# First layer of a two-layer graph attention kernel: half of a chunk's second contexts is issued ahead of the sums of the next chunk

## The chip, the cores and the metric

The kernel runs on one core of one Trainium2 chip. The time is the device time of one execution in microseconds (us). Three runs of the kernel before took 4297.36, 4297.43 and 4297.71 us; the median is 4297.43 us.

The core has five engines with a queue each: TensorE (PE in the profile), VectorE (DVE), ScalarE (ACT), GpSimd (POOL) and SyncE (SP, which here only issues transfers). An instruction waits for others by semaphores; the instructions behind it in the same queue wait with it.

## The reference

There are 8 batches of 2048 rows with 256 features, and one adjacency matrix of 2048 by 2048. Each of two layers normalises the rows, applies a ReLU, runs an attention layer over the graph and adds the result to its input. The change is in the first layer, whose attention normalises each chunk of 256 keys on its own:

```python
q = (x @ Wq.T + bq).reshape(B, N, H, Dh).transpose(0, 2, 1, 3)   # H = 4 heads, Dh = 64
...
scores = jnp.einsum('bhnd,bhjcd->bhnjc', q, kc) / jnp.sqrt(jnp.asarray(Dh, dtype=q.dtype))
scores = jnp.clip(scores, -10.0, 10.0)
scores = jnp.where(mask == 0, jnp.asarray(-10.0, scores.dtype), scores)
attn = jax.nn.softmax(scores, axis=-1)            # over the 256 keys of chunk j
ctx = jnp.einsum('bhnjc,bhjcd->bhnd', attn, vc)   # summed over the 8 chunks
out = ctx @ Wo.T + bo
```

After that come a residual and a layer norm. The second layer is an attention with additive scores, a leaky ReLU and one softmax over all keys. The change doesn't touch it.

## The kernel before, in words

**Tiling.** The first layer runs over steps (b, qb, c): batch, block of 512 queries (`QB`), chunk of 256 keys. That is 8 x 4 x 8 = 256 steps, named n. The scores are kept transposed, with keys on the partitions, so a chunk is two tiles of 128 keys (k = 0 and 1), and for each tile there are two pairs of heads (hp): four tiles E of 128 x 1024 a step.

**One step.** The loop that starts near L732 works on three chunks at once. In the order in which a step issues them:

1. `contexts(0)` (L749) multiplies the weights of key tile 0 of chunk n by the values. It calls `weigh` (L456, its matmuls are L460) for part 0 and part 1 (the two halves of each head's 64 values); each part has four heads, and so four matmuls of 32 columns that run beside each other. Part p goes into the PSUM bank `both[p]`.
2. `advance()` may put in a piece of other work: projections to q, k, v and the output projection (L153), transposes of normalised rows (L156), the adjacency masks (L272).
3. `prepared(steps[n + 2])` issues the scores of chunk n + 2: four times `scores` (L435), each two matmuls of 64 rows (L440) into a PSUM pair, and on DVE one clamp with the mask (L448), which writes E and leaves the pair free. ACT then takes the exponentials of the first two E (L454).
4. The sums of chunk n + 1: `add_up` (L468) multiplies the added exponentials by ones, four matmuls of 32 columns (L471), into half of a PSUM pair. `divide` (L475) has ACT copy them to `s` (L478), and SP moves them to a small tile `sum` (L480).
5. The second half of `prepared`: the exponentials of the other two E on ACT, and on POOL two adds (L725) of the first tile's and the second tile's exponentials, for the next step's sums.
6. `contexts(1)` (L762) adds key tile 1 of chunk n into `both`, part 0 and then part 1.
7. `accumulate` (L493): DVE multiplies `both[0]` and `both[1]` by r, the reciprocals of chunk n (L498), and POOL adds the products to the accumulator of the block (L500).
8. `spread` (L483): DVE takes the reciprocals of `sum` (L485), SP writes them to HBM (`inv`, L487) and reads them back, four transfers, spread over the partitions as r (L490). They are used in step n + 1.
9. `advance()` or `tick()` again puts in other work. Rows' statistics on DVE (`row_stats`, L47 and L48) and normalised rows on ACT (L144) come from there too.

**What sets the order.** The order is written out by hand: each engine's queue has its instructions in the order in which the program issues them. `advance` and `tick` step through generators (`aside`, `quiet`) with due times in steps.

**Buffers that matter here.** There are three PSUM pairs (`pair()`), handed out in turn to the scores, the sums and the other work (`aux`); two banks `both`, one buffer each; ten tiles E; two tiles `add`; one tile s and one tile r. A step's four scores and its sums take five pairs in a row, so the fourth scores take the pair of the first, and the sums that of the second.

Of the kernel before, what the change touches and what calls it, by code (L numbers as in the profile page):

```python
# [51 lines left out]
def layers(  # L52
# [40 lines left out]
    def pair(dtype=F32):  # L93
        n = QB if dtype == F32 else 2 * QB
        return psum.tile([P, 2, n], dtype, tag="big", name="big", bufs=3)

    def banks(name):
        return [psum.tile([P, QB], F32, tag=f"both{k}", name=name) for k in range(2)]
# [6 lines left out]
    def heads_tile(name, tag, bufs=2):  # L105
        return big.tile([P, 2, QB], F32, tag=tag, name=name, bufs=bufs)
# [96 lines left out]
    def tick():  # L203
        moved = False
        for steps_of in list(quiet):
            got = next(steps_of, quiet)
            if got is quiet:
                quiet.remove(steps_of)
            moved = moved or got is not False
        return moved  # L210

    def advance(all_of=True):

        moved = all_of and tick()
        for steps_of in list(aside):
            got = next(steps_of, aside)
            if got is aside:
                aside.remove(steps_of)
            moved = moved or got is not False
            if got is None:  # L220
                if here[0] < 0:
                    aside.append(aside.pop(aside.index(steps_of)))
                break
        return moved

    def drain(until=lambda: False):
        while not until() and advance():
            pass
# [54 lines left out]
    def other_limits():  # L283
        for qb in range(1, NQB):
            yield from make_limit(qb)
# [58 lines left out]
    def batch(b):  # L344
        qkv[b] = ([], [], [])
        rstd, off = norm_of[b] = norms()
        mv = small.tile([P, NKT, 2], F32, tag="mv", name="mv", bufs=1)
        ready, turned = [], []

        def slot():  # L350

            n = here[0]
            while b and here[0] < n + 1:
                yield False

        def statistics():

            for blk in range(NQB):
                while (
                    here[0] < first_of(b) + TURN[blk] - 2 or len(turned) < blk  # L360
                    if b
                    else blk > len(turned) + 1
                ):
                    yield False
                xb = load(x[b], blk)
                yield True
                yield from slot()
                for t in range(NT):
                    row_stats(nc, small, mv[:, blk * NT + t, :], xb[:, t, :])
                roots(mv, rstd, off, slice(blk * NT, (blk + 1) * NT))  # L370
                yield from slot()
                ready.append(xb)

        quiet.append(statistics())
        for blk in range(NQB):
            while len(ready) <= blk:
                yield False
            yield from block(b, blk, ready[blk], turned, *qkv[b])
# [77 lines left out]
    def weigh(kt, part, es, vs, both, first):  # L456

        for h in range(H):
            mine = slice(h * DH + 32 * part, h * DH + 32 * part + 32)
            nc.tensor.matmul(  # L460
                both[part][32 * h : 32 * h + 32, :],
                vs[kt // NT][:, kt % NT, mine],
                es[h // 2][:, h % 2, :],
                start=first,
                stop=not first,
            )

    def add_up(es, sums):  # L468

        for h in range(H):  # L470
            nc.tensor.matmul(  # L471
                sums[32 * h : 32 * h + 32, :], ones, es[h // 2][:, h % 2, :], start=True, stop=True
            )

    def divide(sums):  # L475

        s = big.tile([P, QB], F32, tag="s", name="s", bufs=1)
        nc.scalar.copy(s, sums)  # L478
        got = small.tile([P, 16], F32, tag="sum", name="sum")
        nc.sync.dma_start(got, s[0:P:32, :].rearrange("h (j i) -> h j i", i=16))  # L480
        return got

    def spread(got):  # L483

        nc.vector.reciprocal(got, got)  # L485
        held = dram.tile([H, QB], F32, tag="inv", name="inv", bufs=3)
        nc.sync.dma_start(held.rearrange("h (j i) -> (h j) i", i=16), got)  # L487
        r = big.tile([P, QB], F32, tag="r", name="r", bufs=1)
        for h in range(H):
            nc.sync.dma_start(r[32 * h : 32 * h + 32, :], held[h, :].partition_broadcast(32))  # L490
        return r

    def accumulate(acc, both, r, first):  # L493

        to = acc if first else heads_tile("c", "c")

        for part in range(2):
            nc.vector.tensor_tensor(to[:, part, :], both[part], r, ALU.mult)  # L498
        if not first:
            nc.gpsimd.tensor_tensor(acc, acc, to, ALU.add)  # L500
# [187 lines left out]
    def fill(qb):  # L688

        while here[0] < (B - 1) * NQB * NCH + qb * NCH + NCH - 1:  # L690
            yield False
        for two in range(NKT // 2):
            mine = limit[:, qb, 2 * two : 2 * two + 2, :]
            nc.scalar.activation(mine, mine, AF.Relu, scale=2.0 * FULL, saturate=False)
            yield True

    def last_batch():
        yield from batch(B - 1)
        yield from sources_of(W, a)
        yield from preparation(0)  # L700
# [9 lines left out]
    def prepared(step):  # L710


        b, qb, c = step
        drain(lambda: qb in made and b in qkv and len(qkv[b][1]) > c // 2 and len(qkv[b][0]) > qb)
        qs, ks, _ = qkv[b]
        tiles = [[scores(qb, 2 * c + k, hp, qs, ks) for hp in range(2)] for k in range(2)]
        for e in tiles[0]:
            exponential(e)
        yield tiles
        for e in tiles[1]:  # L720
            exponential(e)
        added = []
        for hp in range(2):
            both = heads_tile("add", "add")
            nc.gpsimd.tensor_tensor(both, tiles[0][hp], tiles[1][hp], ALU.add)  # L725
            added.append(both)
        yield added
# [3 lines left out]
    for n in range(-2, len(steps)):  # L731
        here[0] = n  # L732
        if n >= 0:
            b, qb, c = steps[n]
            if n == 0:
                aside.append(other_limits())
            b1 = 1 if n == 1 else b + 2 if (qb, c) == (NQB - 1, NCH - 2) else B
            if b1 < B:
                aside.append(batch(b1) if b1 + 1 < B else last_batch())
            if b == B - 1 and c == NCH - 2:  # L740
                aside.append(fill(qb))
            drain(lambda: len(qkv[b][2]) > c // 2)
            both = banks("both")

            def contexts(k):
                for part in range(2):
                    weigh(2 * c + k, part, weights[n][0][k], qkv[b][2], both, k == 0)

            contexts(0)  # L749

        used[0] = 0
        advance(n < 0)
        coming = prepared(steps[n + 2]) if n + 2 < len(steps) else iter(())
        weights[n + 2] = [next(coming, None)]
        inside = -1 <= n < len(steps) - 1
        if inside:
            sums = pair()[:, 0, :]
            add_up(weights[n + 1][1], sums)
            got = divide(sums)
        weights[n + 2].append(next(coming, None))  # L760
        if n >= 0:
            contexts(1)  # L762
            if c == 0:
                accs[qb] = heads_tile("acc", "acc")
            accumulate(accs[qb], both, r, c == 0)
            weights.pop(n)
            if c == NCH - 1:
                quiet.append(finish(b, qb, accs[qb]))
        if inside:
            r = spread(got)  # L770
        if n < NQB * NCH or used[0] == 0 or qb == NQB - 1 or qb == 0 and c < NCH // 2:
            advance()
        else:
            tick()
# [128 lines left out]
    for s, (k, jt) in enumerate(rounds):  # L903
# [31 lines left out]
        while due and due[0][0] <= s:  # L935
            _, m, parts = due.pop(0)
# [316 lines left out]
```

## Time and profile before

| | |
|---|---|
| median of three runs | 4297.43 us |
| the profiled execution | 4298.93 us, its span 4297.1 us |
| granted TensorE clock | 0.99 of full speed over the span |
| first layer's loop | from about 45 to 2780 us |
| PE / DVE / ACT / POOL busy from 60 to 2780 us | 2639 / 1849 / 1566 / 2138 us of 2720 |
| PE / DVE / ACT / POOL busy from 2780 to 4297 us | 1427 / 1337 / 934 / 1260 us of 1517 |

In a group's line the engine comes after the source line, then the operation with out<-in by the program's names, shapes, how many, busy time, mean duration in ns, and the idle time just ahead of them with what ended it. In a timeline a row has its start, its duration, engine, line, operation and how many records it merges. An fp32 matmul shows as two records, called passes here; the records of matmuls that run side by side start within some ns of each other. A matmul's record of about 0.59 us runs past the start of the next, so gaps on PE are read between starts. PEld is PE's weight load, SPq an issue of a transfer by SP; data land later than the issue ends.

### The profile page before, as it was taken

What the parts mean: (1) busy time and instruction counts of PE and PEld (TensorE: products, weight loads), DVE (VectorE), ACT (ScalarE), POOL (GpSimd) and SP (SyncE); (2) the same over time, 40 slices, a digit from 0 to 9 for tenths busy, and PEclk for the clock granted to TensorE, in tenths of its full rate; (3) what the DMA queues carried; (4) which work ended last, traced back from release to release, by engine and by line L of the source; (5) the groups of instructions that cost most, each with busy time, mean ns of one, the idle gap of its engine ahead of it and who ended that gap; (6) DMA issues with size and microseconds to landing.
All of it is one profiled execution on the core that took longest, in us unless ns stands there. A gap on an engine that the chain in (4) does not pass through costs nothing. (4 is left out here: it accounts for less than half of the span.)

```text
span 4297.1 us, 86491 instructions
## 1 busy us (share of the span) xinstructions
PE 4103.1 (95%) x34742; PEld 1452.8 (34%) x34742; DVE 3221.3 (75%) x3974; ACT 2527.1 (59%) x3194; POOL 3409.1 (79%) x1795
## 2 busy tenths in 40 slices
PE   7889999999999999999999999989999999999998
PEld 3333333333333333333333333323333233333322
DVE  4676766666667666666666567689898898988997
ACT  4555555555655565555555567565666656566665
POOL 2467787887788788788788778878887888887897
PEclk9999999999999999999999999999999999999999
DMA  3221121122112111112211121211221212122121
GB/s 100 81 90 49 47 59 57 47 55 60 47 54 62 49 52 54 57 47 54 61 49 52 59 61 46 86 57 52 60 70 33 75 52 67 53 59 70 33 62 34
DMA packets 280267, 248.16 MB, mean 58 GB/s; under 512 B 95792, under 2 KB 230704, under 8 KB 279856
## 3 DMA queue, kind: packets, MB, share of 16 engines
q1 hardware_dynamic: 275248, 225.76, 18.7%
q0 software_dynamic: 4608, 16.78, 1.0%
q8 instruction: 275, 4.51, 0.5%
q14 instruction: 136, 1.11, 0.1%
HBM read 204.15 MB, written 36.18 MB: 56 GB/s over the span
## 5 line engine op out<-in xcount | busy, mean ns | idle before, releaser
L448 DVE SCALAR_TENSOR_TENSOR E<-big,limit 128x1024 f32<-128x1024 f32 x1024 | 1182.7, 1217 | 653.3 <-PE big L440 647.1
L725 POOL TENSOR_TENSOR add<-E 128x1024 f32<-128x1024 f32 x512 | 1203.5, 2372 | 569.8 <-PE both L460 474.2
L454 ACT ACTIVATE E<-E 128x1024 f32<-128x1024 f32 x1024 | 1055.0, 1057 | 540.3 <-DVE E L448 521.9
L809 DVE SCALAR_TENSOR_TENSOR e<-big,far,limit 128x1024 f32<-128x1024 f32 x1024 | 1239.6, 1275 | 39.5 <-POOL t L928 18.3
L928 POOL TENSOR_TENSOR t<-t,e 128x1024 f32<-128x1024 f32 x448 | 1055.2, 2388 | 226.7 <-ACT t L924 225.6
L820 PE MATMUL acc<-e,qn 128*32 128x512 f32 x8192 | 1035.6, 596 | 5.6 <-DVE e L809 5.5
L440 PE MATMUL big<-qT,kT 64*128 64x512 f32 x4096 | 966.8, 609 | 43.0 <-DVE E L448 35.6
L460 PE MATMUL both<-E,v 128*32 128x512 f32 x8192 | 991.9, 596 | 0.5 <-DVE c L498 0.2
L924 ACT ACTIVATE t<-e,quot 128x1024 f32<-128x1024 f32 x512 | 561.4, 1142 | 267.9 <-PE big L832 165.0
L440 PEld LDWEIGHTS big<-qT,kT 64*128 64x128 f32 x4096 | 366.3, 187 | 589.9 <-issue 384.1
L500 POOL TENSOR_TENSOR acc<-acc,c 128x1024 f32<-128x1024 f32 x224 | 530.3, 2368 | 1.4 <-DVE c L498 1.4
L460 PEld LDWEIGHTS both<-E,v 128*32 128x32 f32 x8192 | 274.9, 110 | 601.8 <-issue 345.7
L820 PEld LDWEIGHTS acc<-e,qn 128*32 128x32 f32 x8192 | 274.5, 110 | 504.8 <-issue 462.0
L832 PE MATMUL big<-t,for_sums 128*32 128x512 f32 x2048 | 359.3, 596 | 62.3 <-POOL t L928 51.1
L498 DVE TENSOR_TENSOR c<-both,r 128x512 f32<-128x512 f32 x448 | 308.8, 690 | 44.3 <-PE both L460 17.3
L471 PE MATMUL big<-add,ones 128*32 128x512 f32 x2048 | 282.7, 610 | 12.2 <-DVE E L448 1.8
L478 ACT COPY s<-big 128x512 f32<-128x512 f32 x256 | 150.1, 586 | 81.2 <-PE big L471 81.1
L832 PEld LDWEIGHTS big<-t,for_sums 128*32 128x32 f32 x2048 | 76.2, 109 | 282.2 <-POOL t L928 172.2
L164 ACT COPY hT<-big 128x512 f32<-128x512 f32 x128 | 74.2, 580 | 135.2 <-PE big L156 135.2
L144 ACT ACTIVATE h<-x,off,rstd 128x256 f32<-128x256 f32 x256 | 139.1, 592 | 4.7 <-POOL off L135 4.7
L337 ACT ACTIVATE qT<-big,bq 128x512 f32<-128x512 f32 x64 | 44.0, 687 | 153.9 <-PE big L153 153.9
L318 ACT COPY v<-big 128x512 f32<-128x512 f32 x64 | 37.4, 584 | 157.4 <-PE big L153 120.1
(116 smaller groups left out, 3122.3 us busy)
## 6 DMA issues: line engine op xcount, KB each, us to landing
r<-inv SPq DMA_DIRECT2D x1024, 64.0 KB
x<-in_x_dram SPq DMA_DIRECT2D x96, 512.0 KB
es<-er SPq DMA_DIRECT2D x64, 512.0 KB
adj_in<-in_adj_dram SPq DMA_DIRECT2D x32, 512.0 KB
x<-o POOLq DMA_DIRECT2D x32, 512.0 KB, 3.3
x<-x SPq DMA_DIRECT2D x32, 512.0 KB
xh<-x SPq DMA_DIRECT2D x64, 256.0 KB
out_dram<-xh SPq DMA_DIRECT2D x64, 256.0 KB
```

The lines of the kernel that those rows point to most:

```text
L440: nc.tensor.matmul(ps[:, hh, :], ks[kt // NT][own, hp, (kt % NT) * P : (kt % NT + 1) * P], qs[qb][own, hp, :], start=True, stop=True,)
L448: nc.vector.scalar_tensor_tensor(e, ps, -0.5, bcast(limit[:, qb, kt, :], 1, 2), ALU.max, ALU.min)
L454: nc.scalar.activation(e, e, AF.Exp, scale=0.25 * EDGE)
L460: nc.tensor.matmul(both[part][32 * h : 32 * h + 32, :], vs[kt // NT][:, kt % NT, mine], es[h // 2][:, h % 2, :], start=first, stop=not first,)
L498: nc.vector.tensor_tensor(to[:, part, :], both[part], r, ALU.mult)
L500: nc.gpsimd.tensor_tensor(acc, acc, to, ALU.add)
L725: nc.gpsimd.tensor_tensor(both, tiles[0][hp], tiles[1][hp], ALU.add)
L809: nc.vector.scalar_tensor_tensor(e, near[hh], far[:, jt, h : h + 1], limit[:, 2 * half : 2 * half + 2, jt, :], ALU.max, ALU.min,)
L820: nc.tensor.matmul(acc[blk][32 * q : 32 * q + 32, :], qn[jt // NT][:, jt % NT, hp * P + 32 * q : hp * P + 32 * q + 32], es[q // 2][:, blk, :],
L832: nc.tensor.matmul(den[32 * q : 32 * q + 32, :], for_sums[:, m, 2 * hp + q // 2, :], ts[q // 2][:, q % 2, :], start=(m == 0 and k == 0), s ...
L924: nc.scalar.activation(t, now[hh], AF.Copy, scale=quot[:, jt // 2, h : h + 1])
L928: nc.gpsimd.tensor_tensor(ts[hh], ts[hh], now[hh], ALU.add)
```

## The change

`contexts` takes the parts that it is to do. Part 0 of the second key tile is issued ahead of the sums of chunk n + 1 (behind the scores of chunk n + 2), and part 1 stays where it was, behind the second half of `prepared`. On PE a step's order goes from scores, sums, part 0, part 1 to scores, part 0, sums, part 1. No matmul is added or taken out, and no other engine's instructions change places.

```diff
             both = banks("both")
 
-            def contexts(k):
-                for part in range(2):
+            def contexts(k, parts=range(2)):
+                for part in parts:
                     weigh(2 * c + k, part, weights[n][0][k], qkv[b][2], both, k == 0)
 
             contexts(0)
...
         inside = -1 <= n < len(steps) - 1
+        if n >= 0:
+            contexts(1, (0,))
         if inside:
             sums = pair()[:, 0, :]
             add_up(weights[n + 1][1], sums)
             got = divide(sums)
         weights[n + 2].append(next(coming, None))
         if n >= 0:
-            contexts(1)
+            contexts(1, (1,))
             if c == 0:
                 accs[qb] = heads_tile("acc", "acc")
             accumulate(accs[qb], both, r, c == 0)
```

## The prediction

> **What bounds the kernel now.** I read the page first, then the timeline of all engines over two steps of the first layer, then the whole first layer step by step. The page (its engine summary and its table of groups) says where time is spent:
>
> ```profile
> PE 4103.1 (95%) x34742; PEld 1452.8 (34%) x34742; DVE 3221.3 (75%) x3974; ACT 2527.1 (59%) x3194; POOL 3409.1 (79%) x1795
> ...
> L460 PE MATMUL both<-E,v 128*32 128x512 f32 x8192 | 991.9, 596 | 0.5 <-DVE c L498 0.2
> ...
> L471 PE MATMUL big<-add,ones 128*32 128x512 f32 x2048 | 282.7, 610 | 12.2 <-DVE E L448 1.8
> L478 ACT COPY s<-big 128x512 f32<-128x512 f32 x256 | 150.1, 586 | 81.2 <-PE big L471 81.1
> ```
>
> TensorE looks full, but its row hides short waits, because a matmul's record runs past the start of the next. So I read starts, in the timeline of the changed loop (start, duration, engine, line):
>
> ```profile
> 1317.74 3.70 PE L440 MATMUL big<-qT,kT 64*128 64x512 f32 x16
> 1318.99 4.62 DVE L448 SCALAR_TENSOR_TENSOR E<-big,limit 128x1024 f32<-128x1024 f32 x4 [1.57 <-PE big L440]
> ...
> 1321.49 1.06 PE L471 MATMUL big<-add,ones 128*32 128x512 f32 x8
> ...
> 1322.35 3.84 PE L460 MATMUL both<-E,v 128*32 128x512 f32 x32
> ...
> 1322.68 0.59 ACT L478 COPY s<-big 128x512 f32<-128x512 f32 x1 [0.25 <-PE big L471]
> ...
> 1323.17 2.01 ACT L454 ACTIVATE E<-E 128x1024 f32<-128x1024 f32 x2
> ...
> 1323.30 0.55 SPq L480 DMA_DIRECT2D sum<-s  x1
> ...
> 1323.52 1.50 DVE L498 TENSOR_TENSOR c<-both,r 128x512 f32<-128x512 f32 x2
> ...
> 1324.26 0.16 PEld L460 LDWEIGHTS both<-E,v 128*32 128x32 f32 x8 [0.89 <-DVE c L498]
> ...
> 1325.13 0.25 DVE L485 RECIPROCAL sum<-sum 128x16 f32<-128x16 f32 x1
> ```
>
> One step of 8.37 us (1317.74 to 1326.11) is a loop over two engines: scores on PE, four E on DVE, two c behind them, and the next contexts(0), which need `both` back from c, then the next scores. PE waits twice. (1) The last scores pass begins at 1317.74 + 3.70 - 0.59 = 1320.85 and the sums at 1321.49: 0.64 later, where passes otherwise follow at 0.43. (2) contexts(0) begins at 1324.26, right after the first c ends (1323.52 + 0.69 = 1324.21), 0.2 us after PE could have.
>
> **What the change moves.** Nothing is added or removed: per step the same four score pairs, four sums and eight contexts matmuls. Four contexts matmuls (one part, 1.72/2 = 0.86 us) go ahead of the four sums. Only PE's order changes; DVE, ACT, POOL and SP issue the same instructions in the same order. What changes for them is when the sums end.
>
> **Gain: the wait ahead of the sums.** The sums take a PSUM pair that the second E of this chunk must leave. E two ends at 1318.99 + 1.13 + 1.22 = 1321.34, and the sums begin 0.147 us later; in nearly all steps it is the same 0.147, so E is what ends this wait. Contexts part 0 needs no such tile: it can start as soon as the scores are out. How soon? The Trainium skill (TensorEngine Tiling (Array Packing), Key Properties) says that a change of tiling mode drains TensorE, and scores (64 rows) to sums or contexts (128 rows by 32 columns) is such a change. Taken as the whole of 0.64, the rule makes the gain zero, as the contexts meet it instead. A step where E two was early shows how much is drain:
>
> ```profile
> 53.91 5.09 PE L440 MATMUL big<-qT,kT 64*128 64x512 f32 x16
> 58.93 1.06 PE L471 MATMUL big<-add,ones 128*32 128x512 f32 x8
> ```
>
> There the last pass starts at 53.91 + 5.09 - 0.59 = 58.41 and the sums 0.52 later (0.52 also in the step at 170.29). So 0.09 is drain and 0.12 the wait for E. I take the row: 0.115 us a step where the gap is 0.635, 0.045 where it is 0.565.
>
> It counts only where nothing later catches it. In 147 of 253 steps contexts(0) follows contexts(1) at once and waits for c (wait 2, 0.2 us), whose time follows from the scores, not from the sums: gain 0. In 106 steps projection, transpose or output work lies between, and PE runs on. Summed over these, the gap above 0.52 is 13.4 us (53 steps at 0.63, 22 at 0.56 to 0.57, 12 at 0.68, five at 0.95); 1 us of that ends in the waits below. Gain: **12.4 us**.
>
> **Loss: everything behind the sums is later by 0.86 - 0.115 = 0.74 us** (0.81 where the gap is 0.565). The chain is: copy of s (ACT, idle and waiting for the sums in 249 of 256 steps), transfer to `sum`, reciprocal, transfer to `inv`, four transfers to r. Two queues stand behind it.
>
> *ACT*: exponentials three and four are behind the copy, so they, and what ACT does after them, move by 0.74. Usually PE doesn't care. It does where the rows of h for a transpose come right behind them:
>
> ```profile
> 2525.87 2.01 ACT L454 ACTIVATE E<-E 128x1024 f32<-128x1024 f32 x2
> ...
> 2527.77 0.58 ACT L164 COPY hT<-big 128x512 f32<-128x512 f32 x1
> 2528.24 1.09 ACT L144 ACTIVATE h<-x,off,rstd 128x256 f32<-128x256 f32 x2
> 2529.34 0.66 PE L156 MATMUL big<-ident,h 128*128 128x128 f32 x4
> ```
>
> ACT runs without a gap from exponential three to the second h (2528.24 + 1.09 = 2529.33), and the transposes begin at 2529.34. I find 14 transposes and 4 projections (waiting for hT) that end such an unbroken ACT run with a margin under 0.1 us: 18 x 0.77 = **13.8 us**. Ten further projections have 0.93 us: free.
>
> *DVE*: the reciprocal is bound by its transfer. In nearly every step it starts 1.84 to 1.93 us after that issue, with DVE idle 0.1 to 0.2 us before it, so it moves by the full 0.74. Normally 2 us of DVE idle follow. But where the statistics of rows (eight instructions, 2.1 us) stand behind it, the next chunk's first E waits:
>
> ```profile
> 1344.54 0.54 SPq L480 DMA_DIRECT2D sum<-s  x1
> ...
> 1346.44 0.25 DVE L485 RECIPROCAL sum<-sum 128x16 f32<-128x16 f32 x1 [0.17 <-DMA sum<-s]
> ...
> 1348.60 0.18 DVE L48 BATCH_NORM_AGGREGATE mv<-st 128x2 f32<-128x6 f32 x1
> 1348.70 2.32 DVE L448 SCALAR_TENSOR_TENSOR E<-big,limit 128x1024 f32<-128x1024 f32 x2
> ```
>
> The scores of that step began at 1347.36, so E could have started at 1347.36 + 1.25 = 1348.61; it starts at 1348.70, straight behind the statistics. Every delay of the reciprocal lands on E, c and the next contexts(0). There are 21 such steps with no slack: 9 x 0.81 + 7 x 0.74 + 5 x 0.70 = 16.0; in six, work between the contexts gives 0.13 back, and in four the transfer is already late (2.2 to 3.3 us) for another reason and may not move: 16.0 - 0.8 - 1.5 = **13.7 us**.
>
> *The rest.* Nine early steps (180 to 300 us) cast the adjacency masks on ACT behind the exponentials; between 0 and 9 x 0.74 = 6.7, taken as 3, as some wait for input. r lands some 2 us after its last issue (estimate from the one step at 1328.29 where the wait on DVE's queue is seen to end at 1330.31); c comes 3.6 us after that issue in a bare step, so 1.6 - 0.74 still covers it. Only four steps with SP held up have less: **1.6 us**. POOL's adds follow exponentials three and four and move by at most 0.74, and so do the sums that take them: the 0.8 us between stays. The accumulator's add (L500) and the output work stand behind POOL's adds, and SP's block loads behind its transfers; PE needs either a step or more later. Without this cover each bare step would pay up to 0.74.
>
> Sum: 13.8 + 13.7 + 3 + 1.6 - 12.4 = **+19.7 us**, all in the first layer; the second only shifts. The profiled execution took 4298.93 us (span 4297.1, 1.8 around it), the runs' median is 4297.43, 0.03% lower; I set the difference onto the median: **4317 us**.
>
> **Rivals.**
> - *Faster.* The 12.4 us come, and the delays don't bite, since ACT and DVE absorb them: 4285. For it: most DVE idle behind the reciprocal is 2 to 5 us. Against it: the 39 sites (18 + 21) with no margin. It decides once under 12.4/0.75 = 16 of the 39 really pay. 0.09.
> - *No change.* About half the sites pay, or part of each: 39 x 0.35 = 14 against 12.4: 4297 to 4302. 0.11.
> - *Drain takes all.* The skill's rule holds in full, gain zero: 4297.4 + 32.1 = 4330. The two steps at 0.52 speak against it. Within the slower side, 0.12.
> - *r becomes the bound* in bare steps (SP's queue delays it past c): with 0.3 us in each of 147 steps on top, 4317 + 44 = 4361. Against it: only two waits of c on r in the trace, 2.0 us in all. 0.04.
>
> **How the numbers follow.** My sum holds 0.64, drain 0.12, r 0.04: slower 0.80. Same (within 0.2% = 8.6 us, about what a measurement of this kernel can tell from no change) 0.11; faster 0.09. Ends: with half of the losses, 16 - 12.4 = +4 (4301); with the masks in full and four contended transfers moved too, +25; with drain, +33. A little past both: 4298 to 4332. Given slower, its own range is 4306 to 4332.
>
> **What would show it.** Right: in the timeline after, contexts (L460 x16) begins 0.52 after the last scores pass, sums follow 0.86 later, and the bare step stays at 8.37 with contexts(0) still released by c; the copy of s, reciprocal and exponentials three and four sit 0.74 later relative to the scores; the 8.30 us step with statistics behind it (1339.06) is followed by one of about 9.2 rather than 8.45; transposes like 2529.34 wait 0.74 for h; steps with work between contexts shorten by 0.1. The second layer's length stays. Wrong: bare steps change in length (then c isn't bound as I say), contexts starts 0.64 after the scores (drain), or the sites without margin keep their times.

## The result and the profile after

The changed kernel takes 4328.72 us (4324.22 to 4329.2, 4 runs) beside 4297.4 for the kernel before on the same chip: ratio 1.007, interval 1.0058 to 1.0083, slower by 31 us where 20 was forecast. Its profiled execution took 4328.3 us with a span of 4326.5, against 4298.93 and 4297.1. The lines of its page (engine summary and table of groups) that answer to those of before:

```profile
PE 4104.7 (95%) x34742; PEld 1391.9 (32%) x34742; DVE 3214.8 (74%) x3974; ACT 2526.0 (58%) x3194; POOL 3409.8 (79%) x1795
...
L460 PE MATMUL both<-E,v 128*32 128x512 f32 x8192 | 1037.9, 600 | 13.2 <-DVE c L498 2.2
...
L478 ACT COPY s<-big 128x512 f32<-128x512 f32 x256 | 150.0, 586 | 273.5 <-PE big L471 273.4
```

The counts are the same and PE, DVE, ACT and POOL are busy within 7 us of before, so nothing was added: the 31 us are waits. (The 46 us more in L460's row are the tail of one more group of records in each step, which overlaps the sums by 0.18 us.) One number stands out. ScalarE stands idle 273 us in front of the copy of `s`, where it stood 81 us before: 192 us more over 256 steps, 0.75 a step. That is the delay of the sums seen from ScalarE. In the timeline, the same step as the one shown before (its scores began at 1317.74 then):

```profile
1333.72 3.70 PE L440 MATMUL big<-qT,kT 64*128 64x512 f32 x16
...
1337.35 1.06 PE L460 MATMUL both<-E,v 128*32 128x512 f32 x8
1338.23 1.04 PE L471 MATMUL big<-add,ones 128*32 128x512 f32 x8
1339.09 3.06 PE L460 MATMUL both<-E,v 128*32 128x512 f32 x24
1339.41 0.59 ACT L478 COPY s<-big 128x512 f32<-128x512 f32 x1 [1.00 <-PE big L471]
...
1341.86 0.25 DVE L485 RECIPROCAL sum<-sum 128x16 f32<-128x16 f32 x1 [0.97 <-DMA sum<-s]
1342.09 3.70 PE L440 MATMUL big<-qT,kT 64*128 64x512 f32 x16
```

The last scores pass starts at 1333.72 + 3.70 - 0.59 = 1336.83 and the contexts 0.52 later (so in 246 of 255 steps), the sums 0.88 behind them. The copy stands 5.69 us after the first scores (4.94 before), the reciprocal 8.14 (7.39): both 0.75 later. The step is still 8.37 us long. Where the eight statistics stand behind the reciprocal, it is not (scores at 1363.21; before, at 1347.36):

```profile
1363.12 0.25 DVE L485 RECIPROCAL sum<-sum 128x16 f32<-128x16 f32 x1 [1.03 <-DMA sum<-s]
1363.21 2.85 PE L440 MATMUL big<-qT,kT 64*128 64x512 f32 x12
...
1365.28 0.18 DVE L48 BATCH_NORM_AGGREGATE mv<-st 128x2 f32<-128x6 f32 x1
1365.38 4.58 DVE L448 SCALAR_TENSOR_TENSOR E<-big,limit 128x1024 f32<-128x1024 f32 x4
1366.61 2.19 ACT L454 ACTIVATE E<-E 128x1024 f32<-128x1024 f32 x2 [3.51 <-DVE E L448]
1366.63 1.13 PE L440 MATMUL big<-qT,kT 64*128 64x512 f32 x4 [0.57 <-DVE E L448]
```

The first E starts 2.17 us after the scores (1.34 before), TensorE runs out of free pairs and waits 0.57 for it, and the step takes 9.26 us in place of 8.45.

I measured every step of the first layer from first scores to next first scores, in both traces, and added up the differences:

| where | forecast | measured |
|---|---|---|
| 21 steps with statistics behind the reciprocal | +13.7 | +17.5 |
| transposes and projections behind the exponentials (18 forecast, 16 found) | +13.8 | +10.4 net of their own gain |
| nine mask steps (180 to 298 us) | +3 | +6.6 |
| four steps at 2479 to 2520 us | 0 | +6.1 |
| r late | +1.6 | not seen (c waits 1.9 us for r, 2.0 before) |
| gain, other steps with work between the contexts | -12.4 | -10.4 |
| rest of the loop | | +1.0 |
| loop | +19.7 | +31.2 |

Start-up is 3.9 us shorter and what lies behind the last scores 2.0 longer, which leaves the 29.4 us between the spans. The start-up isn't the change's doing: the first scores begin at 45.31 us in the profile of before and at 40.9 to 41.8 in those of all other runs, with either order. The part from the last contexts of the first layer to the end is 1518.3 us before and 1520.4 after.

### The profile page after: what moved, and what is told of

It reads as the page before. It is cut to its first block, busy times and chain, and to the rows that moved or that the text cites. A ratio compares the mean times of both kernels' runs of the same rounds, so it can differ in the third digit from the quotient of the medians.

```text
span 4326.5 us, 86491 instructions
## 1 busy us (share of the span) xinstructions
PE 4104.7 (95%) x34742; PEld 1391.9 (32%) x34742; DVE 3214.8 (74%) x3974; ACT 2526.0 (58%) x3194; POOL 3409.8 (79%) x1795
## 5 line engine op out<-in xcount | busy, mean ns | idle before, releaser
L460 PE MATMUL both<-E,v 128*32 128x512 f32 x8192 | 1037.9, 600 | 13.2 <-DVE c L498 2.2
L440 PE MATMUL big<-qT,kT 64*128 64x512 f32 x4096 | 978.5, 613 | 59.8 <-DVE E L448 51.2
L460 PEld LDWEIGHTS both<-E,v 128*32 128x32 f32 x8192 | 221.1, 109 | 683.4 <-issue 420.2
L471 PE MATMUL big<-add,ones 128*32 128x512 f32 x2048 | 272.8, 598 | 0.1
L485 DVE RECIPROCAL sum<-sum 128x16 f32<-128x16 f32 x256 | 64.8, 253 | 279.6 <-DMA sum<-s 279.6
L153 PE MATMUL big<-hT,wk 128*32 128x512 f32 x1024 | 123.5, 602 | 6.2 <-ACT hT L164 4.9
```

Source lines behind the costliest of these rows:

```text
L440: nc.tensor.matmul(ps[:, hh, :], ks[kt // NT][own, hp, (kt % NT) * P : (kt % NT + 1) * P], qs[qb][own, hp, :], start=True, stop=True,)
L460: nc.tensor.matmul(both[part][32 * h : 32 * h + 32, :], vs[kt // NT][:, kt % NT, mine], es[h // 2][:, h % 2, :], start=first, stop=not first,)
```

## Experiments

My theory: the new order gains 0.1 us in steps with work between the contexts, and loses because two queues behind the sums, ScalarE's and VectorE's, have no slack in some 40 places. Its rival: the new order itself (drains, the wait of the contexts) costs time on TensorE, wherever the queues stand. The first two runs each repair one queue and leave TensorE's order as changed.

**One: the copy of s between exponentials three and four.** From the changed kernel:

```
-        for e in tiles[1]:
-            exponential(e)
+        exponential(tiles[1][0])
+        yield
+        exponential(tiles[1][1])
...
             contexts(1, (0,))
         if inside:
             sums = pair()[:, 0, :]
             add_up(weights[n + 1][1], sums)
+        next(coming, None)
+        if inside:
             got = divide(sums)
```

> The changed kernel with one move on ScalarE: the copy of the sums stands behind three of the chunk's four exponentials, not behind two. The copy then starts at about the same time (it waited for the sums with ScalarE idle 1.0 us a step), but only one exponential stands behind it. If late exponentials cost what the prediction put on ScalarE, the sites with transposes and projections right behind the exponentials give back 0.6 to 0.8 us each, 10.4 us in the trace, 1.5 us more at 931 and 1015 us, and most of the 6.6 us of the mask steps: 4310 us, between 4306 and 4317. If the loss sits in the reciprocal alone, it stays at 4328.

Measured: 4311.01 us (10 runs), ratio to before 1.003, 1.002 to 1.004. The row of the page:

```profile
L478 ACT COPY s<-big 128x512 f32<-128x512 f32 x256 | 145.8, 570 | 19.0 <-PE big L471 18.7
```

ScalarE's wait for the sums falls from 273 us to 19, since exponential three now runs in it. The ScalarE places return: the step at 2520.44 of before took 9.49, after the change 10.07, here 9.38, which is 0.11 under before: the bare gain, no longer hidden by the loss. So such a place costs 0.69 (10.07 - 9.38), not 0.58. The four steps at 2479 to 2520 return as well (6.3 us). The statistics steps stay 0.8 longer, and five further steps with statistics behind the reciprocal, which had some 0.5 us to spare before, get 0.7 longer than after the change (the one at 1409.05 of before: 12.22, 12.10, here 12.87), since there the copy itself starts 0.95 later. The nine mask steps don't return: they stay 6.1 us above before, where I had expected most of the 6.6 back. So the total meets the expected 4310 in part by luck, with the four steps, which weren't in that sum, in the place of the masks.

**Two: the reciprocal and its transfers behind the statistics.**

```
-        if inside:
-            r = spread(got)
         if n < NQB * NCH or used[0] == 0 or qb == NQB - 1 or qb == 0 and c < NCH // 2:
             advance()
         else:
             tick()
+        if inside:
+            r = spread(got)
```

> The changed kernel with the reciprocal (and SyncE's transfers for r) issued behind the other work of the step's end, so that the rows' statistics on VectorE run while the sums are in flight. If the loss behind the reciprocal is the statistics that wait for it, the 21 steps (17.5 us in the trace) return to their times of before: about 4311 us, between 4306 and 4320; r comes up to 1.3 us later in those steps, which may cost up to 0.4 us each. If the loss is ScalarE's alone: 4328 or more.

Measured: 4325.17 us (4 runs), ratio 1.0063, 1.0046 to 1.0079: a miss. Some of the steps that it was aimed at return (9.26 to 8.57, 13.02 to 12.10), but others of the 21 get longer (the one at 820.75 of before: 8.48, then 9.76, here 13.38), so together they stay 15.3 us above before. Steps outside the 21 get longer too, by up to 5.3 us (the one at 2146.67 of the changed kernel, 13.98 for 8.65). The waits of the line that makes c, as its list "its engine sat idle before it until" has them (us, times), in the changed kernel:

```profile
  PE both L460: 19.9, 28
  PE big L471: 2.3, 2
  DMA r<-inv: 1.9, 3
```

and in this one:

```profile
  DMA r<-inv: 46.1, 39
  PE both L460: 13.8, 18
```

c now waits 46 us for r in 39 places: the cover that I had counted for r (0.9 us left of 1.6) doesn't hold two microseconds of statistics. A second surprise went the other way: the mask steps at 180.38 and 244.12 us of before fell from 17.75 and 19.32 us to 11.26 and 13.93.

**Three: both moves.**

> Both moves on top of the changed kernel. If the two queues explain the loss and don't overlap, the gain of 12 us is left with a part of the mask steps against it: 4290 to 4297 us, faster than or as fast as the kernel before. If something else costs time (the transfers of r, TensorE's clock), it stays above 4305.

Measured: 4293.14 us (20 runs), ratio 0.999, 0.9983 to 0.9997. The sum comes out as forecast, but not for the reason I gave: some 12 us of it come from the two mask steps, and late r takes about as much back (c waits 38.7 us for r in 38 places). TensorE's order is the changed one in all three runs, so the order itself isn't what costs 31 us; that rival falls. What the order is worth once the queues are changed is read beside run five.

**Four: the late copy alone, in the kernel before.** The first edit without the change: TensorE keeps its old order, exponential three goes ahead of the copy, so the copy of s, its transfer and the reciprocal are later, and no exponential is.

> The kernel before with the copy of the sums behind the third exponential: TensorE's order is untouched, so there is no gain, and no exponential is later; but the copy, and with it the transfer, the reciprocal and r, is 0.84 us later in a plain step. If a late reciprocal alone costs what the prediction says, the 21 steps pay some 0.8 us each: 4313 us, between 4308 and 4318. If lateness matters only through ScalarE's exponentials, it stays at 4297 or falls.

Measured: 4316.68 us (5 runs), ratio 1.0045, 1.0031 to 1.0059. Ten of the 21 statistics steps get 0.81 to 0.84 longer (all 21 together 16.1 us), the ScalarE places stay at their old 9.49 and 8.89. A later copy of s, with nothing else changed on TensorE, costs 19 us.

**Five: the second edit in the kernel before**, as a control for run three.

> The kernel before with one move: the reciprocal and its five transfers are issued behind the statistics and behind the block's own loads, in every step. Theory: this order alone speeds the two early mask steps by 6.3 us each, since the adjacency loads no longer stand behind the transfers to inv and r in SP's queue (-12.5), and one step near the end by 3.4; against it c waits for r where two microseconds of statistics now go ahead of the reciprocal. In the run with both moves the same terms left +21 us for the late r; here the sums are 0.74 earlier, so some 9 such steps pay 0.74 less each: +14. Sum 4297.4 - 12.5 - 3.4 + 14 = 4296 (4288 to 4303), the mask steps at 11.8 and 13.5 us in place of 17.75 and 19.32. Rival: the late r costs nothing by itself and only the later sums made it late: 4281.

Measured: 4297.86 us (12 runs), ratio 0.9999, 0.999 to 1.0008. Mask steps 11.03 and 12.49; c waits 29.3 us for r. Gain and loss cancel, and late r is a cost of its own even with the sums early. Run three has the same second edit with the new order and the late copy: it is 4.7 us faster than this control, though the two intervals overlap a little.

**Six: a double dose**, both parts of contexts(1) ahead of the sums.

```
-            contexts(1, (0,))
+            contexts(1)
         if inside:
...
         if n >= 0:
-            contexts(1, (1,))
```

> The changed kernel with both parts of contexts(1) ahead of the sums: a double dose, the sums 1.6 us later than before in place of 0.74. Theory: every site that paid pays about twice. Statistics sites 17.5 to 36, ScalarE sites 10.4 to 23, mask steps 6.6 to 13, the slow-clock steps 6 to 10, ten projections with 0.93 us to spare pay 0.7 each (7), the gain stays 10.4; and the cover of r in a bare step is used up (1.6 - 1.6 = 0), so bare steps stay at 8.37 or pay up to 0.2. Sum 4297.4 + 79 = 4376 (4360 to 4400). Rival: the losses are thresholds that are met once, and a second 0.86 us finds the engines waiting anyway: 4330 to 4345.

Measured: 4391.3 us (4 runs), ratio 1.0218, 1.0202 to 1.0234: twice as late costs three times as much, 94 us for 31. The paying places pay double (the statistics step 10.11 after 8.45 and 9.26; the ScalarE step 10.92 after 9.49 and 10.07), and places that had 0.8 us to spare now pay too (the projections 11.38 after 10.55 and 10.52; the steps behind the statistics 10.4 to 12.1 after 10.1). Bare steps stay, but for one of 10.12: 8.38, 8.38, 8.50 as the mean of 24. ScalarE waits 477 us ahead of the copy.

**Seven: the second edit in the first 18 steps only, in the kernel before.**

```
-        if inside:
+        late = n < 18
+        if inside and not late:
             r = spread(got)
...
+        if inside and late:
+            r = spread(got)
```

> The kernel before with the reciprocal and its transfers issued last only in the first 18 steps, while adjacency masks are still being fetched. Theory: the two mask steps lose 6.3 us each and the steps beside them change by less than 1, and no step with statistics behind a sum is touched: 4285 (4283 to 4289). Rival: the two long mask steps only hand their wait on to the next fetch: 4295 to 4298.

Measured: 4281.49 us (5 runs), ratio 0.9964, 0.9951 to 0.9978: faster than both kernels, by 16 and by 47 us, and a little below the expected range. Mask steps 11.45 and 12.35. What was in the way shows in the timeline of SP and ScalarE; first the kernel before:

```profile
179.06 0.32 SPq L487 DMA_DIRECT2D inv<-sum  x1
...
180.46 1.72 SPq L490 DMA_DIRECT2D r<-inv  x4
182.22 1.37 SPq L251 DMA_DIRECT2D adj_in<-in_adj_dram  x3
...
186.41 1.04 ACT L257 CAST masks<-adj_in 128x1024 bf16<-128x1024 int32 x1 [6.64 <-DMA adj_in<-in_adj_dram]
```

then this one:

```profile
176.19 1.37 SPq L251 DMA_DIRECT2D adj_in<-in_adj_dram  x3
...
177.68 0.35 SPq L487 DMA_DIRECT2D inv<-sum  x1
...
181.21 1.04 ACT L257 CAST masks<-adj_in 128x1024 bf16<-128x1024 int32 x1 [2.81 <-DMA adj_in<-in_adj_dram]
```

The three adjacency loads stood behind the transfers to inv and r in SP's queue, and those wait for the reciprocal. Issued ahead of them they let the cast start 2.2 us after the step's scores (179.00) in place of 6.0 (180.38), and the hT copy behind it, which TensorE waits for, comes as much sooner. The rest of the 6.3 us, 2.5, is pace: behind TensorE's wait of 5.63 us for hT the step's other eight score records take 3.71 us to the sums and the sums 1.64; here, behind a wait of 1.80, 1.99 and 0.86.

**Eight: runs one and seven together** (changed order, copy third, the second edit in the first 18 steps).

> The changed kernel with the copy of s moved between exponentials three and four, and the reciprocal and its transfers last only in the first 18 steps. Theory: 4311 - 12.5 = 4299 (4295 to 4302). The statistics sites, which pay 0.8 each, stay as they are. Rival: those sites cost less than the late r does, so that this lies well below the run with both moves: under 4290.

Measured: 4291.64 us (20 runs), ratio 0.9987, 0.998 to 0.9994. Below the forecast: I had taken the mask steps' gain as in the kernel before, but run one's were longer (18.90 and 20.36 against 17.75 and 19.32), and all of that goes too: they fall to 12.50 and 13.28, 13.5 us. Of the rest, some 4 us between the two profiles, 3.0 lie in three steps beside them (11.43, 13.11 and 12.54 in run one; 10.67, 11.90 and 11.50 here). Beside run seven it is 10 us slower: with ScalarE's queue repaired and the masks out of the way, the new order still loses at the statistics what it gains elsewhere, and more (between the two profiles, +16.0 us in the 21 steps and +5.8 in the mask steps, against -7.5 in all others).

**Nine: more work for TensorE.** The four steps at 2479 to 2520 us were missing from my sum. In two steps of the changed kernel the first of the second key tile's score pairs is computed three times over into the same tile, where TensorE otherwise stands idle:

```
-        for hh in range(2):
+        times = 3 if here[0] in (193, 225) and kt % 2 == 1 and hp == 0 else 1
+        for hh in (0, 1) * times:
```

> The changed kernel with more work for TensorE, not less: in two of its 254 steps (those whose scores began at 2155.32 and 2498.45 us in the profile of the changed kernel) the third pair of scores is computed three times over into the same tile, 4 matmuls or 1.72 us more, in a stretch where TensorE otherwise idles 2.27 and 3.24 us waiting for the first E. Theory: the slow passes behind these stretches (0.83 us in place of 0.43) come from the idle itself, so with idle cut to about 0.6 and 1.5 they return to 0.43 and the two steps fall from 12.42 and 13.43 to 11.0 and 11.9; the time by some 3 us. Rival: the pace has another cause (transfers that run at the same time, what VectorE does), and the steps stay at 12.4 and 13.4 or grow.

Measured: 4327.24 us, one run, which tells nothing at this size; the trace tells more. The two steps take 11.15 and 11.93 us in place of 12.42 and 13.43. The second one in the timeline of TensorE, in three kernels (in the last one the edit shifts the line numbers by one). The kernel before:

```profile
2483.79 1.13 PE L440 MATMUL big<-qT,kT 64*128 64x512 f32 x4 [1.44 <-DVE E L448]
2485.01 1.06 PE L471 MATMUL big<-add,ones 128*32 128x512 f32 x8
2485.87 3.84 PE L460 MATMUL both<-E,v 128*32 128x512 f32 x32
```

The same in the changed kernel:

```profile
2504.53 1.13 PE L440 MATMUL big<-qT,kT 64*128 64x512 f32 x4 [3.24 <-DVE E L448]
2505.59 1.87 PE L460 MATMUL both<-E,v 128*32 128x512 f32 x8
2507.22 1.95 PE L471 MATMUL big<-add,ones 128*32 128x512 f32 x8
2508.93 3.02 PE L460 MATMUL both<-E,v 128*32 128x512 f32 x24
```

And with the repeated scores:

```profile
2506.30 1.13 PE L441 MATMUL big<-qT,kT 64*128 64x512 f32 x4 [1.52 <-DVE E L449]
2507.36 1.06 PE L461 MATMUL both<-E,v 128*32 128x512 f32 x8
2508.24 1.04 PE L472 MATMUL big<-add,ones 128*32 128x512 f32 x8
```

And the granted clock in windows over the 5 us that follow (PEclk is the third value from the end), first of the changed kernel:

```profile
2504.50:2509.50 5.00, 4.97 (x28) 1.35 (x32) 3.97 (x4) 2.33 (x3) 0.00 (x0) 0.66 0.01 3
```

and with the repeated scores:

```profile
2506.30:2511.30 5.00, 4.85 (x40) 1.39 (x44) 4.60 (x5) 3.97 (x5) 0.21 (x1) 1.00 0.00 0
```

Eight sums take 0.86 us after an idle of 1.44 or 1.52, and 1.71 after 3.24. With 1.72 us of useless work in the idle stretch the clock stays at 1.00 and the step is 1.5 us shorter. A third step returns without an edit of its own: in the changed kernel the one at 2525.93 stands behind a wait of 1.61 us for h, its scores take 5.40 us and the step 10.92; here the wait is 1.47, the scores take 3.70 and the step 9.23 (9.27 before).

So the slow passes go with the idle, but its length alone doesn't decide. Where neither kernel was edited, the same wait of 2.31 us was followed by the full pace in the changed kernel (granted clock 1.00 over the next 5 us):

```profile
956.84 0.93 PE L156 MATMUL big<-ident,h 128*128 128x128 f32 x4 [2.31 <-ACT h L144]
957.70 3.70 PE L440 MATMUL big<-qT,kT 64*128 64x512 f32 x16
```

and by the slow one in this run (0.66), which costs the step 1.5 us:

```profile
959.56 0.93 PE L156 MATMUL big<-ident,h 128*128 128x128 f32 x4 [2.31 <-ACT h L144]
960.42 5.38 PE L441 MATMUL big<-qT,kT 64*128 64x512 f32 x16
```

With one execution of each kernel in these traces, the 2.27 us of the other edited step may have been such a case. The page *TensorE: Matmul & The Clock Gate* of the Trainium skill (What's actually happening) has such a state at half the clock, entered after an idle window of about 3.4 us. The pace agrees (0.83 to 0.86 for 0.43); the recorded idle ahead of it was shorter here, 1.61 to 3.24 us.

## Why the prediction was right, and where its sizes were off

*The gain was right.* The contexts begin 0.52 after the last scores pass in 246 of 255 steps, as the two early ones had shown: 0.43 pace, 0.09 for the change of mode, and 0.12 of wait for E that is gone. The whole 0.64 as drain is refuted. The 10.4 us of the table leave out the gain inside places that also lose; with 0.11 more in most of the 16 ScalarE places it is close to the 12.4.

*The delay was right*: 0.75 against 0.74, in both queues, and bare steps unchanged. Runs one and four show the two losses apart, as the forecast had them.

*Statistics steps, 17.5 for 13.7.* Fourteen of the 21 pay 0.53 to 0.90, 10.7 together. The surplus is in four steps: the one at 820.75 (1.28), two (931.75 and 1015.74) where statistics and transposes are both behind the sum and each step pays 1.5, and the one at 2139.49, which pays 2.55. The last is one of the four whose transfer was late already and, as I had put it, "may not move". It moved in all four. Three steps stay within 0.1 all the same, so they fit the forecast for another reason: their first E is 0.6 to 0.8 later too, but in the kernel before their sums also waited for POOL's adds, a wait that the part of contexts ahead of the sums now largely fills. In the fourth, two block loads are issued in front of the transfer, as in the kernel before, but now nearer to it (1.86 us ahead for 2.84):

```profile
2149.38 1.70 SPq L490 DMA_DIRECT2D r<-inv  x4
2151.12 0.98 SPq L110 DMA_DIRECT2D x<-in_x_dram  x2
...
2152.98 0.56 SPq L480 DMA_DIRECT2D sum<-s  x1
...
2156.92 0.25 DVE L485 RECIPROCAL sum<-sum 128x16 f32<-128x16 f32 x1 [2.92 <-DMA sum<-s]
```

From issue to reciprocal it is 3.94 us (3.32 before, 1.84 to 1.93 elsewhere). The loads stand behind r's transfers, and these are 1.7 us later in their step, the next sum only 0.76; so the loads come nearer to it. In the other three steps the loads are 2.8 to 3.0 us ahead and the transfer takes 2.2 to 2.5. That the loads are what slows the sum I read from the order in time only; no run took them away. What follows is the idle of 2.27 us and the slow passes, which are gone in run nine: 1.26 of the 2.55.

*ScalarE, 0.69 a place for 0.77, 16 places for 18.* In the transposes shown, the four began at the end of the second h before (2529.34); after, they begin at 2554.72, 0.4 us ahead of its end, so part of the delay finds cover.

*Masks, 6.6 for 3.* The sum meets the upper bound of 6.7, but by luck: the nine steps moved by -0.10 to +1.64, not by 0.74 each. Run one, with the exponentials ahead of the casts early again, keeps 6.1 of it; run eight, with the loads out of r's way as well, has 5.8 us more in these steps than run seven. Which wait it is stays open.

*The missed term, 6.1.* The step that failed is that POOL's adds "move by at most 0.74" and that what stands behind them is needed by TensorE only "a step or more later". The rows of the kernel before, whose next scores begin at 2479.50:

```profile
2473.09 1.93 PE L471 MATMUL big<-add,ones 128*32 128x512 f32 x8
...
2476.78 4.69 POOL L725 TENSOR_TENSOR add<-E 128x1024 f32<-128x1024 f32 x2 [6.66 <-PE both L460]
...
2482.52 4.61 DVE L448 SCALAR_TENSOR_TENSOR E<-big,limit 128x1024 f32<-128x1024 f32 x4
```

and after, where they begin at 2498.45:

```profile
2490.29 2.08 PE L440 MATMUL big<-qT,kT 64*128 64x512 f32 x4 [9.04 <-DVE E L448]
...
2492.30 1.93 PE L460 MATMUL both<-E,v 128*32 128x512 f32 x8
...
2494.00 1.77 PE L471 MATMUL big<-add,ones 128*32 128x512 f32 x8
...
2497.54 4.67 POOL L725 TENSOR_TENSOR add<-E 128x1024 f32<-128x1024 f32 x2 [8.21 <-ACT E L454]
...
2503.26 4.61 DVE L448 SCALAR_TENSOR_TENSOR E<-big,limit 128x1024 f32<-128x1024 f32 x4
```

TensorE had come out of an idle of 9.04 us and ran at half pace, so the one contexts part ahead of the sums took 1.70 us (2492.30 to 2494.00), not 0.86. Measured from the next scores, POOL's adds came 1.81 us later than before, and the first E, which stands on VectorE behind work on products that POOL makes after these adds, 1.79 later (4.81 for 3.02). TensorE idled 3.24 instead of 1.44, and its passes were slow again. The delay grew from 0.74 to 3.3 us in one step; 1.66 of the 6.1 are the slow scores at 2525.93 that run nine shows.

The likeliest case and its mechanism held; the total was 12 us low, mainly through the statistics (+3.8), the masks (+3.6) and the missed term (+6.1), with the ScalarE places (-3.4) against them. The total lies 3 us from the upper end of the range.

## What to carry to other kernels

An operation moved ahead on an engine that looks full is paid for by everything queued behind what it overtakes: list the first waiter on each other engine, and what stands behind that waiter, before counting the gain. A delay isn't a constant: here it doubled while TensorE was at half pace, and by lengthening an idle stretch it could bring that pace about. And look at what a cheap DMA with a late input blocks in its queue: in this kernel five small transfers in front of the adjacency loads cost 16 us, the slow passes behind the longer waits included.

## What the runs showed of the hardware that I had not expected

- TensorE's passes slowed from 0.43 to 0.83 us or more behind idle stretches of 1.61, 2.27 and 3.24 us and didn't behind 1.44, 1.47 and 1.52; behind 2.31 they slowed in one execution and not in another. Where repeated work filled two of these stretches, the steps were 1.26 and 1.50 us shorter.
- A change from scores to sums or contexts cost 0.09 us (0.52 for a pace of 0.43, in 246 of 255 steps of the changed kernel).
- The transfer of `s` to `sum` (128x16 f32, 8 KB), 1.84 to 1.93 us from issue to use, took 3.9 with two block loads issued 1.9 us before it, and 2.2 to 2.5 in three steps with such loads 2.8 to 3.0 us before it.
